# A graph layer on one core: h in two float32r parts instead of three bf16 parts, counts in a ring of three half blocks

## The chip, the cores and the metric

The kernel runs on one core of a Trainium2 chip. The metric is the device time of one execution in microseconds (us). The kernel before took 511.15 us (median of 3 runs, 510.1 to 515.61). The profiled execution took 511.06 us.

Engines are named as in the profile: PE is TensorE (PEld its weight loads), DVE is VectorE, ACT is ScalarE, POOL is GpSimd, SP is the engine whose queue issues most of the DMAs.

## The reference

There are 6250 nodes with 64 features and 206250 edges, sorted by their destination `dst`, with 64 features each. In short:

```python
h   = maximum(layernorm(x), 0)
msg = h[src] + edge_attr_64                      # one row per edge
agg = segment_sum(msg, dst, 6250)                # sum of the rows that end in a node
out = x + relu(agg @ W1 + b1) @ W2 + b2          # 64 -> 128 -> 64
```

Everything is float32. The matrix work of the last line is small; the cost lies in gathering `h[src]` and in summing by node.

## The kernel before

**Counting instead of gathering.** For most nodes no row of h is gathered. For each window of V = 3 neighbouring nodes, whose edges fit into 128 slots, the kernel builds two one-hot matrices on DVE (L702): `hot_lo` is the low 7 bits of each slot's source node, `hot_key` is the pair (which of the three nodes, which of HI = 49 high parts of the source). Their product on PE (L712) gives `pc`, the number of edges from each source to each of the three nodes. A step (`count`) does ST = 6 windows; the one-hots are built for two steps at a time. ACT (L714) copies 882 counts per partition from PSUM to `counts`, laid out as (high part, node). Steps are grouped in blocks of 14: 84 windows, 252 nodes. There are NW = 22 blocks and 310 steps, two of which hold NX = 12 second windows for nodes whose edges need more than 128 slots; these stand at the end of block SB = 8.

**The product with h.** The sum of h over a block's edges is 49 products over the high part: `h3[:, h]` (128 sources by their features) times `counts[:, h]` (128 sources by 252 nodes). h is held as three bf16 parts that add up to it. The first two are one 128-column matrix, so one matmul yields both (L747, the wide products); the third is 64 columns wide, and products of even and odd h go to the two halves of the array (L750, the narrow products). The two halves of the result, partitions 0 to 63 and 64 to 127, are added only in the layer, where W1 stands twice. `counts` has two buffers, one per block, so block b is multiplied while block b + 1 is counted (`multiply_to`): wide products in the steps of `wide_at`, narrow ones in those of `narrow_at`.

**Edge features.** Chunks of 42 nodes, two to a unit: `load` fetches a unit's rows (2 x 384 KB, SP's queue), `chunk_hot` builds its one-hots on DVE (L384), `chunk_sum` sums on PE into `bank` (L396), ACT copies it to `by_node` (L399) and then the fetch of the unit after the next is queued; `chunk_place` puts the 42 columns in their place in the block's `pv` (L408). A block has three units, summed at steps 3, 7 and 11 of the next block and placed at 7, 11 and 13.

**Gathered groups.** The edges of the last nodes are not counted: GP = 24 groups of 1024 edges. Their features are loaded, POOL adds rows of h to them by indirect DMA (eight a group, 192 in all, L256), and PE sums a pair of groups (L425, L429), 42 nodes wide; two adds on DVE (L418) bring it into `sums`.

**The layer.** `add_products` (L759) adds `pv` to `sums`. `mlp_hidden`, `mlp_product`, `mlp_add` and `mlp_store` do a block's two products and store it; x (with b2 added beforehand) is held whole in `xs`.

**Order.** All instructions are in an order written out by hand: the loop over steps puts the pieces above at fixed steps (`before`, `later`, `places`). Each engine works in order. When POOL's next gather is put into the order, and when a pair of groups is summed, follows a plan in us with the constants HEAD_US, STEP_US, GATHER_US, WORDS_US, OPENING_US. Two PSUM buffers hold `pc`, two SBUF buffers each the one-hots.

Of the kernel before, what the change touches and what calls it, by code (L numbers as in the profile page):

```python
# [11 lines left out]
I32 = mybir.dt.int32  # L12
I16 = mybir.dt.int16
# [24 lines left out]
W = 42  # L38
# [10 lines left out]
WR = 128  # L49
WR_BITS = 7  # L50
# [4 lines left out]
GP = 24  # L55
# [13 lines left out]
NX = 12  # L69
BT = 84  # L70
BN = V * BT
NW = 22
NWIN = NW * BT
# [3 lines left out]
SB = 8  # L77
DST_BITS = 13
# [8 lines left out]
assert NC * CN == NS and BN % CN == 0 and CV * V == CN and NX % ST == 0  # L87
# [9 lines left out]
HEAD_US = 1.7  # L97
STEP_US = 1.35
GATHER_US = 2.12
WORDS_US = 2.6  # L100
# [4 lines left out]
OPENING_US = 8.0  # L105
# [3 lines left out]
def gnn_kernel(ctx: ExitStack, tc: tile.TileContext, x, src_t, dst_t, dst_g, edge, w1, b1, w2, b2, out):  # L109
# [3 lines left out]
    start = [b * BN for b in range(NB)] + [N]  # L113
# [12 lines left out]
    agg = consts.tile([P, ACOLS], F32, name="sums")  # L126
# [5 lines left out]
    pools = [tc.tile_pool(name=n, bufs=1, reuse_waits="tile") for n in ("lists", "other")]  # L132
    pr = pools[0].__enter__()
# [10 lines left out]

    firstp_i = small.tile([1, GP], I32, name="firstp_i")
    nc.scalar.dma_start(firstp_i.rearrange("o (q h k) -> o q h k", h=2, k=1),
                        dst_g[GA // 2:G // 2, :, 0:1].unsqueeze(0))
    xl = consts.tile([P, HI + 1, D], F32, tag="x", name="xl")
# [19 lines left out]
    nc.scalar.activation(agg, zero.to_broadcast([P, ACOLS]), AF.Copy)  # L168
# [23 lines left out]
    edge_w = small.tile([P, 4], F32, name="edge_w")  # L192
    for k, of in enumerate((1.0 - W, 0.5, WQ - 0.5, SPAN - 0.5)):
        nc.gpsimd.memset(edge_w[:, k:k + 1], of)
# [16 lines left out]
    select = consts.tile([P, W], F32, name="select")  # L211
    nc.gpsimd.memset(select, 1.0)
    for q in range(JQ):
        part = select[q * QP:(q + 1) * QP, :]
        nc.gpsimd.affine_select(part, part, pattern=[[1, W]], compare_op=OP.is_equal, fill=0.0, base=-QS[q],
                                channel_multiplier=-1)
        nc.gpsimd.affine_select(part, part, pattern=[[0, W]], compare_op=OP.is_ge, fill=0.0, base=WQ - 1,
                                channel_multiplier=-1)
# [45 lines left out]
    def fetch_row(i):  # L264
        rows_of[i] = small.tile([P, L1], I32, name="rows", bufs=6)
        gather(rows_of[i], dst_g.rearrange("q h (r k) -> (q h r) k", k=L1), row_i[:, i:i + 1])

    def seek(i0, n):
        for i in range(i0, i0 + n):

            inrow = small.tile([P, L1], BF16, name="inrow", bufs=2)
            nc.scalar.activation(inrow, rows_of[i], AF.Sign, bias=nhalf[:, i:i + 1], accum_out=first[:, i, 1:2])  # L272
# [9 lines left out]
    dst_p = consts.tile([P, GP, J], I32, name="dst_p")  # L282
    rel_p = dst_p.bitcast(F32)
# [8 lines left out]
    def chunk_starts(c0, c1, tag="po", bufs=1):  # L292
# [6 lines left out]
        known["s", c0] = px  # L299

    def chunk_rows(c0, c1):
        px = known.pop(("s", c0))
        s = starts[:, c0:c1]
        nc.vector.tensor_scalar(s, px[:1, :c1 - c0], float(G * P * J - CE), None, op0=OP.min)
        nc.vector.tensor_copy(starts_i[:, c0:c1], s)

    def chunk_columns(t0, t1, tag="po", bufs=1):
# [12 lines left out]
        known["t", t0] = px  # L320

    def chunk_index(t0, t1):
        px = known.pop(("t", t0))
        nc.vector.tensor_copy(cols_i[:, t0:t1], px[:, t0:t1])

        nc.vector.tensor_scalar(cols[:, t0:t1], px[:, t0:t1], -float(CN), float(CN * EA), op0=OP.mult, op1=OP.add)
        if t0 == 0:
            nc.vector.tensor_copy(cols[:, NT:], px[:, NT:])
# [35 lines left out]
    assert sum(n for _, _, n in units) == NC  # L364

# [35 lines left out]

    def chunk_place(u):
        b, c, n = units[u]
        o = (NX * V if b == SB else 0) - start[b]
        of = by_node.pop(u)
        for i in range(n):
            a = (c + i) * CN + o
            nc.tensor.matmul(pvs[b][0][i * D:(i + 1) * D, a:a + CN], of[:, i, :], select, start=False, stop=False)  # L408

# [3 lines left out]
    def add_sums():  # L413
        for g, pa in to_add:
            for b in range(GB):
                done_at[g + b] = max(made)
                to = agg[:, ds(bases.pop(g + b), W)]
                nc.vector.tensor_tensor(to, to, pa[:, b, :], op=OP.add)  # L418
        to_add.clear()

    def sum_groups(g, tiles):
        pa = bank[:, :GB * W].rearrange("p (b w) -> p b w", b=GB)
        for b in range(GB):
            hot = work.tile([P, J, W], F32, tag="hot", name="hotp")
            nc.vector.tensor_tensor(hot, rel_p[:, g - GA + b, :].unsqueeze(2).to_broadcast([P, J, W]),  # L425
                                    iota[:, :W].unsqueeze(1).to_broadcast([P, J, W]), op=OP.is_equal)
            for j in range(J):
                k = j % 2 * D
                nc.tensor.matmul(pa[k:k + D, b, :], tiles[b][:, j, :], hot[:, j, :],  # L429
                                 start=(j < 2), stop=(j >= J - 2))  # L430
        sum_p = work.tile([P, GB, W], F32, name="sum_p", bufs=1)
        nc.scalar.activation(sum_p, pa, AF.Copy)
# [23 lines left out]
    def norm_center(k):  # L456
        h0, h1 = thirds[k]
        nc.vector.tensor_tensor(xh[:, h0:h1], xh[:, h0:h1], wide(mean, h0, h1), op=OP.subtract)
        part = counts[0].rearrange("p h n -> p (h n)").bitcast(F32)[:, h0 * D:h1 * D]
        part = part.rearrange("p (h d) -> p h d", d=D)  # L460
# [19 lines left out]
    def norm_h(k):  # L480
# [3 lines left out]
        nc.scalar.activation(h3[:, h0:h1, :D], xh[:, h0:h1], AF.Copy)  # L484

    def norm_b(k):
        h0, h1 = thirds[k]
        nc.vector.tensor_tensor(xh[:, h0:h1], xh[:, h0:h1], h3[:, h0:h1, :D], op=OP.subtract)
        nc.scalar.activation(h3[:, h0:h1, D:2 * D], xh[:, h0:h1], AF.Copy)

    def norm_c(k):
        h0, h1 = thirds[k]
        nc.vector.tensor_tensor(h3[:, h0:h1, 2 * D:], xh[:, h0:h1], h3[:, h0:h1, D:2 * D], op=OP.subtract)
# [12 lines left out]
    firstp = small.tile([1, GP], F32, name="firstp")  # L506
    nc.vector.tensor_copy(firstp, firstp_i)
    pe = ps.tile([P, GP], F32, tag="po", name="pe", bufs=1)
    nc.tensor.matmul(pe, ones[0:1, :], firstp, start=True, stop=True)
    nc.scalar.activation(row2[:, GA:], pe, AF.Copy)  # L510
# [20 lines left out]
    pools[0].__exit__(None, None, None)  # L531
    counts.append(ctx.enter_context(pools[1]).tile([P, HI, BN + NX * V], BF16, name="counts1"))
# [11 lines left out]
    b2s = consts.tile([NP, D], F32, name="b2s")  # L544
    nc.sync.dma_start(b2s, b2.partition_broadcast(NP))
    src_p = consts.tile([P, GP * J], I32, name="src_p")
    nc.sync.dma_start(src_p, src_t[:, GA * J:])
    nc.sync.dma_start(dst_p, dst_t.rearrange("p (g j) -> p g j", j=J)[:, GA:, :])

    def table_rows(index, tmp):  # L550
# [3 lines left out]
        nc.vector.scalar_tensor_tensor(index, index, float(HI), tmp, op0=OP.mult, op1=OP.add)  # L554

    def find_groups():

        nc.vector.tensor_scalar(base_i[:, GA:], row2[0:1, GA:], 0.0, float(N - 1), op0=OP.max, op1=OP.min)
        nc.vector.tensor_tensor(rel_p, dst_p, row2[:, GA:].unsqueeze(2).to_broadcast([P, GP, J]), op=OP.subtract)
# [46 lines left out]
    def turn_pair(i0):  # L606
        n = min(2, IC - i0)
        end = min(n * P, NWIN - i0 * P)
        mid = min(max(SB * BT - i0 * P, 0), end)
# [6 lines left out]
    def second_flags():  # L616
# [14 lines left out]
        return lambda: second_ranks(flag, prk, rank, one)  # L631

    def second_ranks(flag, prk, rank, one):
        nc.vector.scalar_tensor_tensor(rank, prk, 1.0, flag, op0=OP.add, op1=OP.mult)
        pick = late.tile([P, IC, NX], F32, tag="part", name="pick")
# [3 lines left out]
        px, pn = pxn[:, :2], pxn[:, 2:]  # L639
        for i in range(IC):  # L640
# [3 lines left out]
        return lambda: second_words(px, pn)  # L644

    def second_words(px, pn):
        second_i = small.tile([NX, 1], I32, name="second_i")
        nc.vector.tensor_copy(second_i, px[:NX, 1:2])
        nc.vector.tensor_scalar(second_b, px[:NX, 0:1], float(SPAN), None, op0=OP.subtract)
        nc.vector.tensor_scalar(second_n, pn[:1, :], float(DUMP), float(DUMP), op0=OP.add, op1=OP.min)  # L650
# [5 lines left out]
    bad = small.tile([P, 9], F32, name="bad")  # L656
    found = small.tile([1, 5], F32, name="found")

    def outside(k):
        over = late.tile([P, NWIN + NX], BF16, tag="part", name="over")[:, :GP * J]  # L660
        nc.scalar.activation(over, rel_p.rearrange("p g j -> p (g j)"), AF.Relu, scale=1.0 if k else -1.0,
                             bias=edge_w[:, 0:1] if k else 0.0, accum_out=bad[:, k:k + 1])

    def inside(n):
        which, k = divmod(n, 2)
        a = (keys[:, 1, :, 0], rel[:, :NC].rearrange("p c q k -> p (c q k)"))[which]
        over = late.tile([P, NWIN + NX], BF16, tag="part", name="over")[:, :a.shape[1]]
        nc.scalar.activation(over, a, AF.Sign, scale=-1.0 if k else 1.0,  # L668
                             bias=edge_w[:, (1, 3 - which)[k]:(2, 4 - which)[k]], accum_out=bad[:, n + 2:n + 3])

    def limits():
        nc.vector.tensor_reduce(bad[:, 6:9], bad[:, :6].rearrange("p (n k) -> p n k", k=2), AX.X, OP.add)
        nc.vector.tensor_tensor(needed, row2[0:1, GA:], needed, op=OP.is_lt)
        nc.vector.tensor_reduce(found[:, 3:4], needed, AX.X, OP.max)
# [484 lines left out]
```

## Time and profile before

| what | value |
|---|---|
| median of 3 runs | 511.15 us |
| profiled execution | 511.06 us |
| its span, first to last instruction | 509.4 us |
| mean granted TensorE clock | 0.991 |
| first eviction of counts starts | 42.0 us |
| first wide product starts | 63.0 us |
| last eviction of counts starts | 483.6 us |
| evictions (L714), mean of one | 310, 908 ns |
| wide and narrow products, mean of one | 1078 at 271 ns, 1078 at 274 ns |
| gathers on POOL, mean of one | 192, 1882 ns |

The span is the time from the first to the last instruction; the execution's time is 1.66 us longer. A matmul's duration in the profile reaches from its start to its modelled end, so neighbours overlap; what one costs in a row of matmuls is the distance of the starts.

### The profile page before, as it was taken

The page shows a single profiled execution, that of the slowest core. Times are in us where ns is not written, and L with a number is a line of the kernel's source. Part 1 is how long each engine was busy: PE and PEld are TensorE (multiplying, and loading weights), DVE is VectorE, ACT ScalarE, POOL GpSimd, SP SyncE. Part 2 cuts the span into 40 slices and gives each one's busy share as a digit, 9 for nine tenths or more (in the row PEclk, how much of TensorE's full clock was granted, in tenths as well). Part 3 has the DMA queues.
Part 4 walks back from the last instruction along what each step waited for, and adds up shares of the span by engine and source line. Part 5 has one row for each costly group of instructions (what it writes and reads, how often), then busy time and mean ns, then how long its engine had stood idle before and what let it go on. Part 6 is the DMA issues. An engine that isn't in the chain of part 4 may idle for free.

```text
span 509.4 us, 19099 instructions
## 1 busy us (share of the span) xinstructions
PE 442.5 (87%) x8183; PEld 380.9 (75%) x8184; DVE 416.8 (82%) x632; ACT 359.1 (71%) x530; POOL 412.0 (81%) x265
## 2 busy tenths in 40 slices
PE   1226678889999988989989999999999999999893
PEld 1115557778888877778878888888888988888782
DVE  4789999698999969979879879799698798698521
ACT  6648867678777656997757777767777777667611
POOL 6676888888874888889888888888888888898880
PEclk9999899999999999999999999999999999999997
DMA  8848722566686566565665676586675766846560
GB/s 235 250 127 276 204 31 59 118 166 165 170 219 188 141 153 161 140 144 163 146 173 108 145 191 145 147 191 147 152 188 144 194 148 140 200 105 153 118 146 17
DMA packets 113544, 79.04 MB, mean 155 GB/s; under 512 B 32920, under 2 KB 108686, under 8 KB 113230
## 3 DMA queue, kind: packets, MB, share of 16 engines
q1 hardware_dynamic: 83962, 65.99, 43.5%
q0 software_dynamic: 29200, 10.25, 17.0%
q10 hardware_dynamic: 292, 1.52, 1.0%
q8 instruction: 66, 1.08, 0.9%
q14 instruction: 24, 0.20, 0.1%
HBM read 73.74 MB, written 3.99 MB: 153 GB/s over the span
## 4 chain that ended last, share of the span: by engine, by line
PE 69%; DVE 17%; issue 4%; ACT 4%; DMA 3%; POOL 1%; DVEq 0%; ACTq 0%; POOLq 0%
PE pc L712 21%; PE pv L747 19%; PE pv L750 11%; PE bank L396 9%; DVE hot_key L702 6%; DVE hot_lo L702 5%; PE pv L408 3%; PE ph L799 2%; PE po L806 2%; PE bank L429 2%; ACT counts L714 2%; DMA rows<-in_dst_g,row_i 1%; DMA dstq<-in_dst_g,cols_i 1%; ACT over L668 1%; POOL rows L256 1%
## 5 line engine op out<-in xcount | busy, mean ns | idle before, releaser
L256 POOL DMA_INDIRECT pfeat<-table,src_p x192 | 361.4, 1882 | 61.3 <-issue 55.2
L714 ACT ACTIVATE counts<-pc 128x882 bf16<-128x882 f32 x310 | 276.8, 908 | 48.5 <-PE pc L712 33.9
L712 PE MATMUL pc<-hot_key,hot_lo 128*128 128x147 bf16 x1860 | 174.0, 231 | 25.8 <-DVE hot_key L702 13.8
L712 PEld LDWEIGHTS <-hot_lo 128*128 128x128 bf16 x1860 | 134.2, 99 | 49.3 <-DVE hot_key L702 18.1
L702 DVE TENSOR_TENSOR hot_lo<-iota_lo,keys 128x1536 bf16<-128x1536 bf16 x155 | 147.9, 954 | 26.6 <-PE pc L712 26.0
L702 DVE TENSOR_TENSOR hot_key<-iota_key,keys 128x1776 bf16<-128x1776 bf16 x155 | 167.0, 1078 | 0.0
L747 PE MATMUL pv<-counts,h 128*128 128x252 bf16 (+1 forms) x1078 | 147.8, 271 | 0.1
L747 PEld LDWEIGHTS <-h 128*128 128x128 bf16 x1078 | 98.7, 97 | 8.0 <-issue 0.2
L750 PE MATMUL pv<-counts,h 128*64 128x252 bf16 (+1 forms) x1078 | 75.4, 274 | 0.0
L399 ACT ACTIVATE by_node<-bank 128x128 f32<-128x128 f32 x66 | 18.4, 278 | 58.2 <-PE bank L396 58.2
L396 PE MATMUL bank<-feat,hot 128*21 128x64 f32 x3168 | 58.6, 223 | 0.7 <-DVE hot L384 0.7
L396 PEld LDWEIGHTS bank<-feat,hot 128*21 128x21 f32 x3168 | 47.2, 102 | 13.7 <-issue 10.7
L750 PEld LDWEIGHTS <-h 128*64 128x64 bf16 x1078 | 53.9, 111 | 3.3 <-issue 0.2
L384 DVE TENSOR_TENSOR hot<-rel,iota 128x504 f32<-128x504 bf16 x66 | 44.8, 679 | 6.4 <-PE bank L429 5.5
L425 DVE TENSOR_TENSOR hotp<-dst_p,iota 128x336 f32<-128x336 f32 x24 | 11.7, 504 | 17.4 <-PE bank L396 17.2
L256 POOL DMA_INDIRECT words<-packed,first_i x15 | 20.5, 1367 | 4.6 <-issue 3.7
L256 POOL DMA_INDIRECT rows<-in_dst_g,row_i x15 | 17.0, 1132 | 8.7 <-ACT inrow L272 3.0
L408 PE MATMUL pv<-select,by_node 128*64 128x42 f32 x264 | 21.1, 243 | 0.0
L408 PEld LDWEIGHTS pv<-select,by_node 128*64 128x64 f32 x264 | 13.2, 136 | 8.3 <-issue 0.6
L801 ACT ACTIVATE hid<-ph,b1s 128x252 f32<-128x252 f32 (+1 forms) x25 | 11.7, 466 | 8.4 <-PE ph L799 7.2
L759 DVE TENSOR_TENSOR sums<-sums,pv 128x252 f32<-128x252 f32 x22 | 9.0, 411 | 9.6 <-PE pv L750 9.6
L799 PE MATMUL ph<-sums,w1s 128*128 128x252 f32 (+1 forms) x50 | 15.4, 390 | 1.6 <-DVE sums L418 1.1
(172 smaller groups left out, 259.0 us busy)
## 6 DMA issues: line engine op xcount, KB each, us to landing
feat<-in_edge SPq DMA_DIRECT2D x132, 384.0 KB
pfeat<-in_edge SPq DMA_DIRECT2D x24, 256.0 KB
pfeat<-table,src_p POOLq DMA_INDIRECT x192
out_y<-y SPq DMA_DIRECT2D x24, 63.0 KB
xs<-in_x SPq DMA_DIRECT2D x4, 315.0 KB
dstn<-in_dst_g SPq DMA_DIRECT2D x1, 1024.0 KB
table<-xl SPq DMA_DIRECT2D x2, 512.0 KB
packed<-dstn ACTq DMA_DIRECT2D x1, 768.0 KB
```

What stands on the lines that cost most here:

```text
L256: nc.gpsimd.indirect_dma_start(out=rows, out_offset=None, in_=source, in_offset=bass.IndirectOffsetOnAxis(ap=index, axis=0), compute_op=op)
L384: nc.vector.tensor_tensor(hot_of[u][:, :n].rearrange("p c j w -> p (c j) w"), rel[:, c:c + n].rearrange("p c q k -> p (c q k)").unsqueeze( ...
L396: nc.tensor.matmul(bank[q * QP:q * QP + WQ, i * D:(i + 1) * D], hot[:, i, j, :], feat[i][:, j, :], start=(k == 0), stop=(k == JP - 1))
L399: nc.scalar.activation(by_node[u][:, :n].rearrange("p c d -> p (c d)"), bank[:, :n * D], AF.Copy)
L408: nc.tensor.matmul(pvs[b][0][i * D:(i + 1) * D, a:a + CN], of[:, i, :], select, start=False, stop=False)
L425: nc.vector.tensor_tensor(hot, rel_p[:, g - GA + b, :].unsqueeze(2).to_broadcast([P, J, W]), iota[:, :W].unsqueeze(1).to_broadcast([P, J, ...
L702: nc.vector.tensor_tensor(hot.rearrange("p t (m o) -> p t m o", o=2), iota_k.rearrange("p (m o) -> p m o", o=2).unsqueeze(1).to_broadcast( ...
L712: nc.tensor.matmul(pc[:, k, m * K:(m + 1) * K], hot_lo[:, j, :], hot_key[:, j, :K], start=True, stop=True)
L714: nc.scalar.activation(counts[b % 2][:, :, s * ST * V:(s + 1) * ST * V].rearrange("p h (k m) -> p h k m", k=2), pc[:, :, :ST // 2 * K].rea ...
L747: nc.tensor.matmul(pv, h3[:, h, :2 * D], of, start=(h == 0 and not clear), stop=False)
L750: nc.tensor.matmul(pv[k:k + D, :], h3[:, h, 2 * D:], of, start=False, stop=(h >= HI - 2))
L799: nc.tensor.matmul(ph[:, :n], w1s, agg[:, start[b]:start[b + 1]], start=True, stop=True)
```

## The change

- h is held as two float32r parts in `h2` (a rounded one and its remainder), side by side in 128 columns. Each block has 49 products of 252 columns; the narrow ones are gone. One residue pass (`norm_low`) replaces two.
- `counts` is float32r, in a ring of three half blocks of 126 nodes, 7 steps each. Block b lies in two of the three. Its products are done in steps 0 to 6 of block b + 1 (`PRODUCTS`), before step 7 writes into the first half's place. In every third block the halves lie in reverse order, and `column` and `add_products` allow for it.
- Units are summed at steps 7, 9, 11 and placed at 9, 11, 13; their one-hots are built two steps earlier. Layers start at steps 7 and 10 instead of 0 and 8.
- 23 blocks are counted (322 steps; NX = 14 second windows within block 8) and GP = 18 groups gathered. A group's edges are arranged by quarters of 32 partitions, so that a pair is summed as a unit is (21 nodes a quarter) and then placed by a computed selection, 52 nodes wide. A group's load is four DMAs instead of one.
- b2 is added by a one-row product; x is fetched block by block in `mlp_hidden`.
- `sums` is cleared by ACT in steps 15 to 21 rather than at the start. Several small results in PSUM are read by ACT rather than DVE.
- The plan's constants change.

```diff
-GP = 24
+GP = 18
+PQ = 4
+PK = J // PQ
-NX = 12
+NX = 14
-NW = 22
+NH = BN // 2
+NW = 23
-HEAD_US = 1.7
-STEP_US = 1.35
-GATHER_US = 2.12
-WORDS_US = 2.6
+HEAD_US = 1.5
+STEP_US = 1.2
+GATHER_US = 2.2
+WORDS_US = 2.9
-OPENING_US = 8.0
+OPENING_US = 3.0
...
-    h3 = consts.tile([P, HI, 3 * D], BF16, name="h3")
-    counts = [consts.tile([P, HI, BN + NX * V], BF16, name="counts0")]
+    h2 = consts.tile([P, HI, 2 * D], F32R, name="h2")
...
+        ring = ctx.enter_context(pools["ring"]).tile([P, 3, HI, NH], F32R, name="counts")
...
+    def norm_low(k):
         h0, h1 = thirds[k]
-        nc.vector.tensor_tensor(h3[:, h0:h1, 2 * D:], xh[:, h0:h1], h3[:, h0:h1, D:2 * D], op=OP.subtract)
+        nc.vector.tensor_tensor(h2[:, h0:h1, D:], xh[:, h0:h1], h2[:, h0:h1, :D], op=OP.subtract)
...
+    for q in range(PQ):
+        nc.tensor.matmul(pe[q * QP:(q + 1) * QP, 1, :], ones[0:1, :QP], firstp[:, :, q], start=True, stop=True)
+    nc.scalar.activation(row2[:, GA:], pe[:, 0, :], AF.Copy)
+    nc.vector.tensor_tensor(off_p, pe[:, 1, :], row2[:, GA:], op=OP.subtract)
...
+        half, i = divmod(s, STEPS // 2)
         nc.scalar.activation(
-            counts[b % 2][:, :, s * ST * V:(s + 1) * ST * V].rearrange("p h (k m) -> p h k m", k=2),
+            ring[:, (2 * b + half) % 3, :, i * ST * V:(i + 1) * ST * V].rearrange("p h (k m) -> p h k m", k=2),
             pc[:, :, :ST // 2 * K].rearrange("p k (m h) -> p h k m", h=HI), AF.Copy)
...
-        h = i % HI
-        of = counts[b % 2][:, h, :pv.shape[1]]
-        if i < HI:
-            nc.tensor.matmul(pv, h3[:, h, :2 * D], of, start=(h == 0 and not clear), stop=False)
-        else:
-            k = h % 2 * D
-            nc.tensor.matmul(pv[k:k + D, :], h3[:, h, 2 * D:], of, start=False, stop=(h >= HI - 2))
+        pv, done, clear = pvs[b]
+        a, z = sorted(((2 * b) % 3, (2 * b + 1) % 3))
+        of = ring[:, a:z + 1:z - a]
+        for h in range(done, upto):
+            nc.tensor.matmul(pv.rearrange("p (k n) -> p k n", k=2), h2[:, h, :], of[:, :, h, :],
+                             start=(h == 0 and not clear), stop=(h == HI - 1 and unplaced[b] == 0))
...
+        hot = work.tile([P, GB, J, WQ], F32, tag="hot", name="hotp")
...
+            for k in range(PK):
+                for q in range(PQ):
+                    j = q * PK + k
+                    nc.tensor.matmul(bank[q * QP:q * QP + WQ, b * D:(b + 1) * D], hot[:, b, j, :],
+                                     tiles[b][:, j, :], start=(k == 0), stop=(k == PK - 1))
...
+    def residual(b):
+        xs[b] = work.tile([NP, 2, D], F32, name="xs", bufs=3)
+        nc.sync.dma_start(xs[b][:pairs[b]], x[start[b]:start[b + 1], :].rearrange("(p k) d -> p k d", k=2))
...
+            nc.tensor.matmul(po[:pairs[b], k, :], ones[0:1, :pairs[b]], b2s, start=True, stop=False)
...
-        nc.sync.dma_start(parts_of[g].rearrange("p j d -> p (j d)"),
-                          edge[g * P * J:(g + 1) * P * J, :].rearrange("(p j) d -> p (j d)", j=J))
+            for b in range(PQ):
+                nc.sync.dma_start(parts_of[g][b * QP:(b + 1) * QP].rearrange("p (q k) d -> p q (k d)", k=PK), rows[b])
...
-    SUMS, PLACES = (3, 7, 11), (7, 11, 13)
+    SUMS, PLACES, LAYERS = (7, 9, 11), (9, 11, 13), (7, 10)
+    PRODUCTS = (5, 12, 19, 26, 33, 41, HI)
...
-        if s in (0, 8) and ready:
+        if s in LAYERS and ready:
             mlp(ready.pop(0), n)
```

More of the change, by code (lines that the diff above doesn't have):

```diff
@@ L37 @@
 GB = 2
-W = 42
+W = 52
 CN = 42
@@ L110, in gnn_kernel @@
     nc = tc.nc
-    start = [b * BN for b in range(NB)] + [N]
+    start = [b * BN - (NX * V if b > SB else 0) for b in range(NB)] + [N]
     pairs = [(start[b + 1] - start[b]) // 2 for b in range(NB)]
@@ L364, in gnn_kernel @@
     assert sum(n for _, _, n in units) == NC
+    unplaced = [sum(1 for unit in units if unit[0] == b) for b in range(NW)]
     def load(u):
@@ L413, in add_sums @@
     def add_sums():
-        for g, pa in to_add:
+        for g, placed in to_add:
             for b in range(GB):
                 done_at[g + b] = max(made)
-                to = agg[:, ds(bases.pop(g + b), W)]
-                nc.vector.tensor_tensor(to, to, pa[:, b, :], op=OP.add)
+                half = slice(b * D, (b + 1) * D)
+                to = agg[half, ds(bases.pop(g + b), W)]
+                nc.vector.tensor_tensor(to, to, placed[half, :], op=OP.add)
         to_add.clear()
-    def sum_groups(g, tiles):
-        pa = bank[:, :GB * W].rearrange("p (b w) -> p b w", b=GB)
-        for b in range(GB):
[L424 to L432, printed above, removed]
@@ new lines, in place_groups @@
+    def place_groups(g):
+        of = by_node.pop(("h", g))
+        placed = ps.tile([P, W], F32, tag="po", name="placed", bufs=1)
+        sel = work.tile([P, GB, W], F32, name="sel", bufs=1)
+        nc.vector.tensor_tensor(sel, iota_wr.unsqueeze(1).to_broadcast([P, GB, W]),
+                                off_p[:, g - GA:g - GA + GB].unsqueeze(2).to_broadcast([P, GB, W]), op=OP.is_equal)
+        for b in range(GB):
+            nc.tensor.matmul(placed[b * D:(b + 1) * D, :], of[:, b, :], sel[:, b, :], start=True, stop=True)
+        sum_p = work.tile([P, W], F32, name="sum_p", bufs=1)
+        nc.scalar.activation(sum_p, placed, AF.Copy)
@@ new lines, in gnn_kernel, with by_quarters @@
+    nc.sync.dma_start(src_s.rearrange("p g b k -> p (g b k)"), src_t[:, GA * J:])
+    dst_s = early.tile([GP * PQ, PK * P], I32, name="dst_s")
+    nc.sync.dma_start(dst_s, dst_g.rearrange("q h (r k) -> (q h r) k", k=PK * P)[GA * PQ:G * PQ, :])
+    src_p = consts.tile([P, GP, PQ, PK], I32, name="src_p")
+    def by_quarters():
+        px = ps.tile([P, PQ, GP, PK], F32, tag="po", name="psrcq", bufs=1)
+        rows = src_s.bitcast(F32)
+        for q in range(PQ):
+            for b in range(PQ):
+                nc.tensor.matmul(px[b * QP:(b + 1) * QP, q], ident[:, q * QP:(q + 1) * QP], rows[:, :, b, :],
+                                 start=True, stop=True)
+        nc.scalar.activation(src_p.rearrange("p g q k -> p q g k"), px, AF.Copy)
@@ L562, in gnn_kernel, with turn_groups @@
+    def turn_groups():
+        rel_s = known.pop("g")
+        pt = ps.tile([P, PK, GP * PQ], F32, tag="po", name="pgrp", bufs=1)
+        for k in range(PK):
+            nc.tensor.transpose(pt[:, k, :], rel_s[:, k], ident[:GP * PQ, :GP * PQ])
+        nc.scalar.activation(rel_p.rearrange("p g q k -> p (g q) k"), pt.rearrange("p k r -> p r k"), AF.Copy)
     behind = small.tile([P, IC], F32, name="behind")
@@ L630, in second_flags, with second_ranks @@
                              start=False, stop=(i == IC - 2))
[L631 to L635, printed above, removed]
+        nc.scalar.activation(rank, prk, AF.Copy)
+        return lambda: second_ranks(flag, rank, one)
+    def second_ranks(flag, rank, one):
+        nc.vector.scalar_tensor_tensor(rank, rank, 1.0, flag, op0=OP.add, op1=OP.mult)
+        pick = late.tile([P, IC, NX], F32, tag="dstq", bufs=2, name="pick")
         nc.vector.tensor_tensor(pick, rank.unsqueeze(2).to_broadcast([P, IC, NX]),
@@ L666, in inside @@
         a = (keys[:, 1, :, 0], rel[:, :NC].rearrange("p c q k -> p (c q k)"))[which]
-        over = late.tile([P, NWIN + NX], BF16, tag="part", name="over")[:, :a.shape[1]]
-        nc.scalar.activation(over, a, AF.Sign, scale=-1.0 if k else 1.0,
-                             bias=edge_w[:, (1, 3 - which)[k]:(2, 4 - which)[k]], accum_out=bad[:, n + 2:n + 3])
+        m = -(-a.shape[1] // CHECKS)
+        for i in range(CHECKS):
+            of = a[:, i * m:(i + 1) * m]
+            over = late.tile([P, 2 * CQ], BF16, tag="dstq", bufs=2, name="over")[:, :of.shape[1]]
+            at = bad[:, 4 + (which * CHECKS + i) * 2 + k:][:, :1]
+            nc.scalar.activation(over, of, AF.Sign, scale=-1.0 if k else 1.0,
+                                 bias=edge_w[:, (1, 3 - which)[k]:(2, 4 - which)[k]], accum_out=at)
@@ L805, in mlp_product @@
         for k in range(2):
[L806 removed]
+            nc.tensor.matmul(po[:pairs[b], k, :], ones[0:1, :pairs[b]], b2s, start=True, stop=False)
+            nc.tensor.matmul(po[:pairs[b], k, :], outs[b][:, k:2 * pairs[b]:2], w2s, start=False, stop=True)
         y = work.tile([NP, 2, D], F32, name="y")
@@ L876, in gnn_kernel @@
     load(1)
-    for g in range(GA + 2, GA + 4):
-        load_h(g)
+    open_ring()
     todo = {}
```

340 lines of the change are left out of this document (175 added, 165 removed).

## The prediction

> **What bounds the kernel now.** The page first: shares of the span, and the engines on the chain that ended last.
>
> ```profile
> PE 442.5 (87%) x8183; PEld 380.9 (75%) x8184; DVE 416.8 (82%) x632; ACT 359.1 (71%) x530; POOL 412.0 (81%) x265
> ...
> PE 69%; DVE 17%; issue 4%; ACT 4%; DMA 3%; POOL 1%; DVEq 0%; ACTq 0%; POOLq 0%
> ```
>
> An average over stages, so next the busy times by stretches of 40 us (columns: stretch, length, then PE, PEld, DVE, ACT, POOL, the granted clock, DMA share, GB/s).
>
> ```profile
> 160.00:200.00 40.00, 36.80 (x729) 31.75 (x721) 35.61 (x59) 26.12 (x40) 34.21 (x20) 1.00 0.68 171
> ...
> 280.00:320.00 40.00, 40.00 (x749) 35.07 (x747) 33.96 (x46) 30.58 (x45) 34.51 (x19) 1.00 0.69 165
> 320.00:360.00 40.00, 40.00 (x748) 35.11 (x746) 34.26 (x46) 30.28 (x46) 34.20 (x20) 1.00 0.69 165
> ```
>
> From 280 on TensorE has no idle time; VectorE has 15%, ScalarE a quarter. POOL's rest is the 0.3 us between gathers, so it too runs end to end. The timeline of one stretch gives what each PE piece costs: not its duration, which holds the drain, but from its start to the next start.
>
> ```profile
> 341.38 0.32 PE L408 MATMUL pv<-select,by_node 128*64 128x42 f32 x4
> ...
> 341.52 0.83 PE L750 MATMUL pv<-counts,h 128*64 128x252 bf16 x12
> ...
> 342.28 0.87 PE L396 MATMUL bank<-feat,hot 128*21 128x64 f32 x48
> ...
> 343.08 0.56 PE L712 MATMUL pc<-hot_key,hot_lo 128*128 128x147 bf16 x6
> ...
> 343.48 0.70 PE L747 MATMUL pv<-counts,h 128*128 128x252 bf16 x5
> ...
> 344.02 0.55 PE L712 MATMUL pc<-hot_key,hot_lo 128*128 128x147 bf16 x6
> ...
> 345.80 0.64 PE L799 MATMUL ph<-sums,w1s 128*128 128x252 f32 x2
> ```
>
> Placing 0.14, 12 narrow products 0.76 (63 ns each), a unit of edge features 0.80, five wide products 0.54 (108 ns each), a step's counting 0.40 and, up to the next start at 344.50, 0.48. The float32 product of the layer is two instructions, and the next start (346.27) is 0.47 later. A block of 14 steps: counting 14 x 0.44 = 6.2, wide 49 x 0.108 = 5.3, narrow 49 x 0.063 = 3.1, units 3 x 0.80 = 2.4, placing 0.4, layer 0.47 + 0.41 = 0.9, gathered groups 12 pairs x 1.06 / 22 = 0.6: 18.9 us. Measured from 280 to 400: 526 counting matmuls, at 84 a block 6.26 blocks, 19.2 us each. So 0.3 is switching, and the block's length is PE's sum.
>
> **The product.** The change drops the narrow products (3.1 a block) and replaces 49 wide bf16 ones by 49 float32r ones of the same 128x128 and 252 columns. No row has float32r. From below it costs what bf16 does, 108 ns; from above what float32 does, 0.47 us. I take 108: h is split in two parts of this type, which would be pointless if a product kept all of float32's digits; a type that needs a second part does not need float32's passes. A single instruction of the float32 pair (0.235) lies between and is a rival. The weights are four bytes wide too. The timeline of weight loads at a float32 transpose:
>
> ```profile
> 106.12 0.14 PEld L593 LDWEIGHTS pk<-ident,klo 128*128 128x128 f32 x1
> 106.19 0.14 PEld L594 LDWEIGHTS pk<-ident,khif 128*128 128x128 f32 x1
> 106.30 0.14 PEld L593 LDWEIGHTS pk<-ident,klo 128*128 128x128 f32 x1
> 106.41 0.14 PEld L594 LDWEIGHTS pk<-ident,khif 128*128 128x128 f32 x1
> ```
>
> They follow each other by 0.11 us with matmuls running beside them, so a wide float32 load just fits under 108 ns of streaming.
>
> **PE after, per block.** Counting 6.2, products 5.3, units 2.4, placing 0.4; the layer 0.9 plus the bias as two one-row products (four instructions, about 0.1 each as po's four take 0.41), times 25/23: 1.4; groups 9 pairs x (0.55 for 32 instructions at the units' 0.80/48, plus 0.14 for placing) / 23 = 0.3; switching 0.3. Sum 16.3, 2.9 under today's 19.2.
>
> **What is late next: VectorE.** Pairs of one-hots start 0.87 and 0.99 after each other in the chain of waits: 7 x 1.86 = 13.0 a block. Unit one-hots 3 x 0.6, add of products 0.33 (in a third of the blocks two adds: 0.4), layer add 0.25, groups 9 x (0.45 + 0.25 + 0.35) / 23 = 0.4: 15.9. So PE and DVE come out level and the halves of a block decide. The ring has three half blocks, so all products of a block must be done in the next one's steps 0 to 6, and units and layers move to 7 to 13. First half: PE 3.1 + 5.3 + 0.3 = 8.7, DVE 6.5 + 0.6 + 0.4 + 0.2 = 7.7. Second: PE 3.1 + 2.4 + 0.4 + 1.4 + 0.3 = 7.6, DVE 6.5 + 1.2 + 0.25 + 0.2 = 8.15. The larger of each: 16.85; the two one-hot buffers could even it out to 16.3. The eviction writes four bytes for two. ScalarE from PSUM takes 277 ns for 128 float32 elements and 908 for the 882 to bf16, 0.84 ns an element, and from SBUF 1063 to float32 against 1061 to bf16 for 1024: width costs nothing. Its block is 15 us (30.3 busy in two blocks), covered; without that cover it would cost what passes 16.9.
>
> **A transfer with less cover.** Units now lie at steps 7, 9, 11 instead of 3, 7, 11, and the third one's features are fetched when the first has been summed: four steps, 4 x 1.21 = 4.8 us. Today's such transfer, queue row and DMA windows:
>
> ```profile
> 342.87 1.00 SPq L375 DMA_DIRECT2D feat<-in_edge  x2
> ```
> ```profile
> 342.90:344.60 1.70, 1.70 (x41) 1.43 (x28) 0.94 (x2) 1.18 (x2) 1.40 (x2) 1.00 0.55 65
> 344.60:347.50 2.90, 2.90 (x39) 2.51 (x40) 2.89 (x4) 2.41 (x4) 2.60 (x2) 1.00 1.09 296
> 347.50:348.50 1.00, 1.00 (x14) 0.96 (x12) 1.00 (x2) 1.00 (x2) 0.69 (x2) 1.00 0.11 14
> ```
>
> The sum began at 342.28 and the bytes stop at 347.5: 5.2 us. A shortage of 0.4, of which DVE's longer second half hides some: 0.25. Block: 17.1. At the queue, each group's load becomes four issues (18 x 4 instead of 24, 0.36 each), and each layer fetches its rows of x; both stand before unit loads, which is the second rival.
>
> **Ends.** Counting begins at 42.0 (first eviction) and the first product at 63.0. In the head the clearing of the sums (5.54 on ScalarE until 9.58, with the cast of src right behind) goes, worth up to 3 us; the offsets' subtraction, which waits for ScalarE's copy of the first nodes, now stands before the two merges of dst, and copies through ScalarE are new: about as much. From -3 to +3, taken as 0. The clearing returns in steps 15 to 21, four times 1.4 us on ScalarE, which is busy 14.2 of 20 us there. From 63.0 to the last eviction's end at 484.5 lie 21 blocks in 421.5, 18 more than 21 x 19.2: lists unpacked, residues of h, second windows. Residues (one pass instead of two) and the b2 adds shrink, 4 us: 14 stay. The tail from 484.5 to 509.4 is 24.9; its narrow run (494.27 to 497.17) goes, and so does the wait for the last gathered nodes' layer (500.75 to 503.57), since 144 gathers of 2.2 us end some 100 us earlier; the last block's rows of x, fetched only at its layer, may come 2 us late: 21.
>
> Sum: 42 + 21 + 22 x 17.1 + 14 + 21 = 474 of span; the profiled execution's 511.06 stands 1.7 over its span, and at the median of 511.15. **476 us.** Own range 455 (blocks at 16.3, head -3) to 497 (blocks at 18).
>
> **Rivals.**
>
> 1. Slower: float32r streams at the pitch of one float32 instruction, 0.235. Place: the 49 products in steps 0 to 6. That half takes 3.1 + 11.5 + 0.3 = 14.9, the block 23.3, the tail 6 more: 42 + 21 + 513 + 5 + 27 + 1.7 = 610 (the early extras mostly hide under PE). It decides from a pitch of about 0.14: 35 us over 23 x 49 products. For it: four-byte rows cost this in every matmul shown. Against: the two parts. Chance 0.11.
> 2. The same place, with loads and streams in turn: 0.11 + 0.108 = 0.218, block 22.5, 591. Against: the five wide bf16 products above, on the same rows of the array, run at 0.108 with a load each. Chance 0.02. [...]
> 3. All of float32's passes: 0.47, block 34.9, 871. The split speaks against it. Chance 0.05.
> 4. The transfer is the bound: a pair of group loads (8 x 0.36 of issue, 512 KB at 296 GB/s, 4.7 us) stands before a third unit's features, seven times, and the 0.4 shows fully: up to 37 more, half likely, 497; the worst case, 513, is no change. For it: the queue works in order. Against: group loads come due anywhere in a block. Chance 0.15.
>
> POOL as the bound is out: 144 x 2.2 = 317 us from 60 on.
>
> **The numbers.** Forecast 0.67, rivals 0.11, 0.02, 0.05, 0.15. Within 1% (506 to 516, as little as a measurement here tells from none) fall 0.05 of the fourth; slower are the first three, 0.18; faster 0.77. The range runs from 450, as the head may give more, to 508, into the fourth case; what is left out is mostly the slow product.
>
> **What would show it.** Product pitch 108 ns in runs of 7; the counting phase near 1.22 us a step; PE under 97% and DVE over 93% between 150 and 430; no wait of the bank's matmuls on features above 1 us; evictions still at 0.91. A pitch over 0.14, or PE full in the first halves of blocks while DVE waits on pc, makes it wrong.

## The result and the profile after

The changed kernel took 542.25 us (median of 4 runs, 538.56 to 543.22) against 510.79 for the kernel before: a ratio of 1.058 with a 95% interval of 1.050 to 1.066. It is slower, outside the forecast's range and on the other side of no change.

The page of the changed kernel: engines' shares, then the engines and lines of the chain that ended last.

```profile
span 540.8 us, 17705 instructions
...
PE 457.6 (85%) x7459; PEld 399.0 (74%) x7460; DVE 419.5 (78%) x639; ACT 371.5 (69%) x582; POOL 333.9 (62%) x222
...
PE 63%; ACT 9%; POOL 7%; DVE 7%; issue 6%; DMA 5%; SPq 1%; DVEq 0%; POOLq 0%; ACTq 0%
PE pv L808 24%; PE pc L788 18%; PE bank L417 7%; ACT counts L791 6%; POOL pfeat L279 5%; PE po L857 3%; PE po L856 3%; DMA feat<-in_edge 3%; PE ph L849 3%; ACT over L743 2%; DVE hot_key L778 2%; PE pv L433 1%; DVE hot_lo L778 1%; DMA pfeat<-table,src_p 1%; POOL words L279 1%
```

PE has some 700 instructions fewer and is busy 15 us longer. Three stretches of 40 us (stretch, length, then PE, PEld, DVE, ACT, POOL, granted clock, DMA share, GB/s):

```profile
240.00:280.00 40.00, 33.69 (x465) 29.37 (x463) 30.25 (x53) 23.40 (x32) 34.08 (x20) 0.87 0.57 132
...
320.00:360.00 40.00, 38.84 (x647) 33.76 (x646) 31.76 (x43) 28.70 (x43) 25.52 (x14) 1.00 0.59 146
360.00:400.00 40.00, 39.48 (x641) 34.22 (x641) 31.57 (x44) 28.74 (x43) 26.96 (x15) 0.97 0.59 146
```

VectorE did not become the bound: between 320 and 400 it is busy 31.6 to 31.8 of 40 us, less than the 34 before, and PE is still nearly full. Between 150 and 430 PE is busy 93% of the time and VectorE 80%, where the forecast had under 97% and over 93%. The timeline of PE shows products in the first half of a block, then a placing and a layer in the second:

```profile
340.95 1.07 PE L808 MATMUL pv<-counts,h 128*128 128x252 f32 x7
...
341.86 0.56 PE L788 MATMUL pc<-hot_key,hot_lo 128*128 128x147 bf16 x6
...
348.03 0.32 PE L433 MATMUL pv<-select,by_node 128*64 128x42 f32 x4
348.31 0.87 PE L417 MATMUL bank<-feat,hot 128*21 128x64 f32 x48
349.11 0.43 PE L856 MATMUL po<-b2s,ones 1*126 1x64 f32 x2
349.46 0.44 PE L857 MATMUL po<-w2s,hid 128*126 128x64 f32 x2
349.84 0.43 PE L856 MATMUL po<-b2s,ones 1*126 1x64 f32 x2
350.20 0.44 PE L857 MATMUL po<-w2s,hid 128*126 128x64 f32 x2
350.52 0.56 PE L788 MATMUL pc<-hot_key,hot_lo 128*128 128x147 bf16 x6
```

Seven products from 340.95 to 341.86: 130 ns each, not 108. A placing, 348.03 to 348.31: 0.28 us for four instructions, where the kernel before took 0.14. The layer's second product with its bias, 349.11 to 350.52: 1.41 us, where the forecast had 0.8 and the kernel before took 0.41:

```profile
348.23 0.57 PE L806 MATMUL po<-w2s,hid 128*126 128x64 f32 x4
348.64 0.56 PE L712 MATMUL pc<-hot_key,hot_lo 128*128 128x147 bf16 x6
```

To see what the sum became, the distances from each PE start to the next were added up by line from 88 us to about the end of counting (516 after, where the last eviction ends at 514.8, and 484.4 before), idle time apart, and divided by the blocks in that time (20.7 after, 20.0 before):

| per block, us | before | forecast | after |
|---|---|---|---|
| counting | 5.9 | 6.2 | 6.2 |
| products with h | 8.4 | 5.3 | 6.6 |
| units | 2.4 | 2.4 | 2.6 |
| placing | 0.4 | 0.4 | 0.8 |
| closing product (L435) | none | not seen | 0.2 |
| layers | 1.0 | 1.4 | 2.1 |
| gathered groups | 0.6 | 0.3 | 0.4 |
| rest and PE's idle time | 1.1 | 0.3 | 1.8 |
| sum | 19.8 | 16.3 | 20.7 |

A few per cent of the records are missing, so the entries are good to some 0.1 us. The halves of a block differ: by the starts of counting on PE, in the seven blocks from 316 to 459 us the first half mostly takes 9.3 us, where the forecast had 8.7, and the second 10.4 to 12.1, where it had 8.15. Placing, closing and the layers stand in the second.

### The profile page after: what moved, and what is told of

Same layout as the page of the kernel before. It is cut to its first block, busy times and chain, and to the rows that moved or that the text cites. A ratio compares the mean times of both kernels' runs of the same rounds, so it can differ in the third digit from the quotient of the medians.

```text
span 540.8 us, 17705 instructions
## 1 busy us (share of the span) xinstructions
PE 457.6 (85%) x7459; PEld 399.0 (74%) x7460; DVE 419.5 (78%) x639; ACT 371.5 (69%) x582; POOL 333.9 (62%) x222
## 4 chain that ended last, share of the span: by engine, by line
PE 63%; ACT 9%; POOL 7%; DVE 7%; issue 6%; DMA 5%; SPq 1%; DVEq 0%; POOLq 0%; ACTq 0%
PE pv L808 24%; PE pc L788 18%; PE bank L417 7%; ACT counts L791 6%; POOL pfeat L279 5%; PE po L857 3%; PE po L856 3%; DMA feat<-in_edge 3%; PE ph L849 3%; ACT over L743 2%; DVE hot_key L778 2%; PE pv L433 1%; DVE hot_lo L778 1%; DMA pfeat<-table,src_p 1%; POOL words L279 1%
## 5 line engine op out<-in xcount | busy, mean ns | idle before, releaser
L791 ACT ACTIVATE counts<-pc 128x882 fp32r<-128x882 f32 x322 | 288.8, 917 | 80.7 <-PE pc L788 75.5
L279 POOL DMA_INDIRECT pfeat<-table,src_p x144 | 279.1, 1938 | 78.0 <-issue 38.7
L788 PE MATMUL pc<-hot_key,hot_lo 128*128 128x147 bf16 x1932 | 183.1, 235 | 26.6 <-DVE hot_key L778 13.0
L808 PE MATMUL pv<-counts,h 128*128 128x252 f32 x1127 | 175.6, 296 | 3.8 <-ACT counts L791 3.1
L808 PEld LDWEIGHTS pv<-counts,h 128*128 128x128 f32 x1127 | 146.5, 193 | 7.4 <-ACT counts L791 6.6
L405 DVE TENSOR_TENSOR hot<-rel,iota 128x504 f32<-128x504 bf16 (+1 forms) x69 | 46.6, 677 | 29.4 <-PE bank L417 27.4
L420 ACT ACTIVATE by_node<-bank 128x128 f32<-128x128 f32 (+1 forms) x69 | 19.3, 279 | 17.1 <-PE bank L417 16.2
L856 PE MATMUL po<-b2s,ones 1*126 1x64 f32 (+2 forms) x100 | 22.2, 303 | 1.2 <-ACT hid L851 1.2
L857 PE MATMUL po<-w2s,hid 128*126 128x64 f32 (+2 forms) x100 | 23.1, 314 | 0.0
L856 PEld LDWEIGHTS po<-b2s,ones 1*126 1x126 f32 (+2 forms) x100 | 15.2, 190 | 6.4 <-ACT hid L851 2.0
L849 PE MATMUL ph<-sums,w1s 128*128 128x252 f32 (+2 forms) x50 | 17.7, 436 | 1.9 <-ACT sum_p L476 0.8
```

What stands on the lines that cost most here:

```text
L279: nc.gpsimd.indirect_dma_start(out=rows, out_offset=None, in_=source, in_offset=bass.IndirectOffsetOnAxis(ap=index, axis=0), compute_op=op)
L405: nc.vector.tensor_tensor(hot_of[u][:, :n].rearrange("p c j w -> p (c j) w"), rel[:, c:c + n].rearrange("p c q k -> p (c q k)").unsqueeze( ...
L420: nc.scalar.activation(by_node[u][:, :n].rearrange("p c d -> p (c d)"), bank[:, :n * D], AF.Copy)
L788: nc.tensor.matmul(pc[:, k, m * K:(m + 1) * K], hot_lo[:, j, :], hot_key[:, j, :K], start=True, stop=True)
L791: nc.scalar.activation(ring[:, (2 * b + half) % 3, :, i * ST * V:(i + 1) * ST * V].rearrange("p h (k m) -> p h k m", k=2), pc[:, :, :ST // ...
L808: nc.tensor.matmul(pv.rearrange("p (k n) -> p k n", k=2), h2[:, h, :], of[:, :, h, :], start=(h == 0 and not clear), stop=(h == HI - 1 and ...
```

## The experiments

The experiments ran in three sets, each on one chip beside the kernel before, whose median was 514.6 us for the first four, 534.5 for the next four and 530.0 for the last two. So only ratios compare across sets. The changed kernel itself was not run again in these sets: that its ratio of 1.058 holds on the other chips is assumed, not shown.

**b2 on VectorE instead of PE.**

```diff
-            nc.tensor.matmul(po[:pairs[b], k, :], ones[0:1, :pairs[b]], b2s, start=True, stop=False)
-            nc.tensor.matmul(po[:pairs[b], k, :], outs[b][:, k:2 * pairs[b]:2], w2s, start=False, stop=True)
+            nc.tensor.matmul(po[:pairs[b], k, :], outs[b][:, k:2 * pairs[b]:2], w2s, start=True, stop=True)
...
+        nc.vector.tensor_tensor(y[:pairs[b]], y[:pairs[b]],
+                                b2s[:pairs[b]].unsqueeze(1).to_broadcast([pairs[b], 2, D]), op=OP.add)
```

> The changed kernel with b2 added on VectorE after the layer's add instead of by a one-row product on PE. Theory: PE paces the kernel, and the two one-row products of a layer cost it about 1.0 us (po took 1.41 us from its first start to the next piece's, against 0.41 before), so 25 layers give back 22 to 25 us: 515 to 522 us. Rival, VectorE paces it (it has 0.2 to 0.3 us a layer more here): 542 to 550.

525.42 us, 1.024 of the kernel before (1.016 to 1.031). Against the change's 1.058 that is 0.034, or 17 us, good to some 6 us by the two intervals: the direction of the theory, about three quarters of its size, in spite of one more instruction a layer on VectorE. PE paces the kernel, VectorE does not.

**The bias product with 128 rows.** Same instructions, other tile.

```diff
-ones[0:1, :pairs[b]], b2s, start=True
+ones[:, :pairs[b]], b2s, start=True
```

> The changed kernel with the one-row product of b2 done with 128 rows (ones times a matrix that holds b2 in its first row and zeros below), so the number of instructions stays and the switch between tiles of 1 row and of 128 rows goes. If the switch is the cost: po's eight instructions at about 0.1 us each, 0.85 for 1.41 us, 14 us less in all: 528 us. If the number of float32 instructions is the cost: po stays at 1.3 to 1.4 us, 540 to 543 us.

535.87 us in one run, 1.041. In the tally of starts an instruction of the bias product costs 124 ns instead of 183 and one of the layer's product beside it 129 instead of 174, which over the run comes to the same 9 us by which this run is shorter. So about half of the bias's cost (9 of 17 us, the first of these from one run) is changing between tiles of one row and of 128, and the rest is the four instructions.

**Products in bf16.** Type alone; h's third part is left out.

```diff
-    h2 = consts.tile([P, HI, 2 * D], F32R, name="h2")
+    h2 = consts.tile([P, HI, 2 * D], BF16, name="h2")
-        ring = ctx.enter_context(pools["ring"]).tile([P, 3, HI, NH], F32R, name="counts")
+        ring = ctx.enter_context(pools["ring"]).tile([P, 3, HI, NH], BF16, name="counts")
```

> The changed kernel with h's two parts and the ring of counts in bf16: the products have the same shape, the same halves and the same place, and h's third bf16 part is left out. Theory, four-byte weights set the pitch of the products: 131 ns falls to 108 to 112, 1.0 us a block: 515 to 520 us. Rival, the pitch comes from reading the two halves of the ring: it stays at 131, 540 to 543 us. If the width of what ScalarE writes counted, its eviction would fall from 917 ns.

527.96 us, 1.026 (1.019 to 1.034). The timeline of PE:

```profile
350.88 0.91 PE L808 MATMUL pv<-counts,h 128*128 128x252 bf16 x7
351.64 0.55 PE L788 MATMUL pc<-hot_key,hot_lo 128*128 128x147 bf16 x6
```

0.76 for seven: 109 ns, against 108 in the kernel before, whose counts of a block lie in one buffer, and 130 in the changed kernel. Reading the two halves of the ring costs 1 ns at most, the type 21. The time gained (0.032, 16 us) is less than 1127 x 21 ns = 24: second halves, where the bias stands, still took 10.4 us or more in most blocks after 270. From 88 us to the end of counting the granted clock also stood at half for 27 us in this run against 20 in the changed kernel's. Evictions: 909 ns against 917, so the width that ScalarE writes is 1%.

**Each product in two halves of 126 columns.**

```diff
-            nc.tensor.matmul(pv.rearrange("p (k n) -> p k n", k=2), h2[:, h, :], of[:, :, h, :],
-                             start=(h == 0 and not clear), stop=(h == HI - 1 and unplaced[b] == 0))
+            for k in range(2):
+                nc.tensor.matmul(pv[:, k * NH:(k + 1) * NH], h2[:, h, :], of[:, k, h, :], start=False, stop=False)
...
```

> The changed kernel with each float32r product split into two of 126 columns, same weights loaded twice (and one zeroing and one closing product of a block more, 4 us in all). If loading 128 columns of four-byte weights sets the pitch, 126 columns stay at about 131 ns: 98 of them take 12.8 us a block instead of 6.4, 680 us. If streaming sets it, 126 columns cost about 65 ns: 545 us.

663.95 us in one run. PE's timeline:

```profile
359.94 1.76 PE L809 MATMUL pv<-counts,h 128*128 128x126 f32 x14
361.54 0.56 PE L788 MATMUL pc<-hot_key,hot_lo 128*128 128x147 bf16 x6
```

114 ns for 126 columns. Half the columns save 16 of 130 ns, so most of the pitch does not go with the columns; what stays the same is the load of 128 columns of weights. PEld's rows are about as long as PE's distances: 0.89 us for the changed kernel's seven loads from 340.92, 1.64 for these fourteen from 359.91. That the load is the floor is argued from this and was not shown: no run changed the load alone. And 131 was not confirmed: 126 columns cost less than 252. Rival 2, load and stream in turn, stood at 0.218 us; 130 ns for 252 columns speaks against it.

**The removal alone, in the kernel before.** 47 of 49 narrow products go; the third part of h is left out for them.

```diff
-        else:
+        elif h >= HI - 2:
             k = h % 2 * D
             nc.tensor.matmul(pv[k:k + D, :], h3[:, h, 2 * D:], of, start=False, stop=(h >= HI - 2))
```

> The kernel before without 47 of the 49 narrow products of each block (the third bf16 part of h is left out for them; the last two stay and close the sum). It is the removal alone. By the prediction's step, PE falls by 3.0 us a block to 16.2 and VectorE is next at 15.9, so a block of 16.3 to 16.9: 22 x 2.3 to 2.9 us less and 2.7 less in the tail, 444 to 458 us. Rival, in-order waits of VectorE on PE take a good part of it: about 485 to 490.

529.77 us (528.01, 531.53, 533.15, 520.83) where the kernel before took 534.47 (529.57 to 539.69): about 1% less by the medians. Two of the four runs lie below all of the kernel before, the other two do not, so no size of a gain is settled; 444 to 458 and 485 to 490 were both missed. PE's waits (engine, line, waited for; us in total, times, longest):

```profile
PE bank L429 <- DMA pfeat<-table,src_p: 23.7, 17, 1.9
PE pc L712 <- DVE hot_key L702: 18.5, 16, 4.7
```

PE now waits for gathered rows, which it never did in the profile before; the last gather starts at 511.1 us (495.2 before). While the gathers kept up, the gain was there: the two blocks from 282 to 316 us took 17.4 and 16.7 us by the starts of counting, against 20.0 and 18.8 for the two from 284 in the kernel before, and the forecast's 16.3 to 16.9. Later three single gathers lasted 7.2 to 9.3 us, PE waited for their groups, and the granted clock was then at half for 10 us each time (from 396, 437 and 478); second halves there took up to 21 us. So the 192 gathers in a row stand about as close to bounding the kernel before as PE does; that fewer gathered groups, and with them a 23rd block, were needed for a larger gain is argued from this. The plan's STEP_US stayed at 1.35, so part of the waits may come from sums placed too early; that was not tested.

**Units at steps 3, 7, 11 again** (with b2 on VectorE).

```diff
-    SUMS, PLACES, LAYERS = (7, 9, 11), (9, 11, 13), (7, 10)
+    SUMS, PLACES, LAYERS = (3, 7, 11), (7, 11, 13), (7, 10)
```

> The kernel with b2 on VectorE, and the units summed at steps 3, 7, 11 and placed at 7, 11, 13 as in the kernel before (their one-hots still two steps earlier), so that each fetch of features has at least four steps with products in them and the last one eight. Theory, PE's waits for features (7.0 us) and the throttling of its clock after them are worth 8 to 15 us: 510 to 517 us where that kernel took 525. Rival, the pieces only move from one PE-bound half to the other: 522 to 528.

545.15 us, 1.018 (1.007 to 1.029), against 1.024 (1.016 to 1.031) with b2 on VectorE alone, on another chip. PE's wait for features is gone from its longest waits, and first halves grew from 9.3 to about 11 us; the intervals overlap. This fits the rival: the waits were real and worth little. The half clock did not go with them (14 us of counting from 88 on, against 17 with b2 on VectorE alone; the profiles' mean clocks are 0.965 and 0.961), so this run does not price it.

**Group loads from ScalarE's queue** (with b2 on VectorE).

```diff
-                nc.sync.dma_start(parts_of[g][b * QP:(b + 1) * QP]
+                nc.scalar.dma_start(parts_of[g][b * QP:(b + 1) * QP]
```

> The kernel with b2 on VectorE, and the loads of the gathered groups issued from ScalarE's queue instead of SP's. If eight group loads standing before a unit's features on SP are what makes PE wait, the wait goes: 513 to 520 us for 525. Rival, issuing on ScalarE holds back evictions by as much: 524 to 530.

572.27 us, 1.073 (1.065 to 1.081): worse than either expectation. ScalarE's waits, and one of its stretches of issuing:

```profile
ACT counts L791 <- PE pc L788: 63.0, 141, 1.3
ACT counts L791 <- DMA pfeat<-in_edge: 24.1, 5, 6.1
```
```profile
231.37 3.87 ACTq L879 DMA_DIRECT2D pfeat<-in_edge  x8
```

The loads held ScalarE up to 6.1 us at a time with evictions queued behind, and PE's two count buffers behind those: counting on PE waited 9.1 us for evictions, up to 3.2 at a time. The wait that the edit was aimed at did shrink: PE waited 1.6 us for features instead of 7.0. Within about 3 us of the end of each hold-up the granted clock went to half for 3.4 to 10.2 us; its mean in this run's profile is 0.898, in the changed kernel's 0.931.

**Both edits.**

> The two edits before this one together (units at 3, 7, 11; group loads from ScalarE's queue; b2 on VectorE). If both waits are separate: 506 to 514 us. If they are the same wait, as one of them alone: 512 to 518.

583.14 us, 1.095 (1.086 to 1.105). ScalarE's hold-ups (26.6 us in 6 waits) are the same, and nothing of the first edit offsets them.

**b2 on VectorE and bf16 products together.** The two diffs above; h's third part is left out.

> The two edits that each gave time back, together: b2 on VectorE, and h's two parts and the counts in bf16 (h's third bf16 part is left out). Alone they took the ratio to the kernel before from 1.058 to 1.024 and to 1.026. If they are separate pieces of one engine's sum, PE's: 0.99 to 0.995 of the kernel before, first halves of a block at 8.3 us and second halves at 8.5 to 10. Rival, VectorE becomes the bound at once (its block is 15.9 us of work without waits): 1.01 to 1.02.

518.15 us (514.18, 513.29, 522.12, 525.92), each below the fastest of the kernel before (530.04, 528.35 to 533.02, 7 runs); the ratio of the medians is 0.978, that of the two shorter runs 0.969, both without an interval. Alone the two edits gave 0.034 and 0.032; together 0.080 or more, at least their sum. Both are terms of PE's sum, one in each half of a block. Part of what goes beyond the sum may be the clock: it stood at half for 7 us of counting from 88 on here, against 17 and 27 with each edit alone. This version beats both kernels, but it keeps two bf16 parts of h instead of three, which is less than either holds.

**Work shared out again: 22 blocks, 26 groups** (with b2 on VectorE, float32r).

```diff
-GP = 18
+GP = 26
-NW = 23
+NW = 22
-STEP_US = 1.2
+STEP_US = 1.38
```

> The kernel with b2 on VectorE (float32r as in the change) and the work shared out again: 22 blocks counted and 26 groups gathered, STEP_US of the plan 1.38. PE has one block less (19 us) and four pairs more (4 us): 1.024 falls by 0.029 to 0.995 of the kernel before. POOL's chain of 208 gathers at 2.2 us from 45 on ends at 503, and the last pair's layer some 10 us later: about 515, 1.00. If POOL is not pressed by anything else: 0.995 to 1.005; if its gathers take longer under the denser traffic: 1.02.

558.48 us, 1.050 (1.043 to 1.058): 5% over the kernel before, where the worst expectation was 2%. The estimate of POOL's chain was too short. In the profile, which is of the longest of the four runs, the 208 gathers start from 47.0 to 542.9 us, 2.40 us apart on average, where the estimate took 2.2 and their end at 503. The 192 of the kernel before start from 44.8 to 495.2, 2.36 apart; by that pace the chain would have ended at about 535. PE waited 14.3 us for gathered rows. That this chain set the length of the run is argued, and no run with faster gathers tests it.

## Why the prediction was wrong

**What paces the changed kernel** is PE, as b2 on VectorE shows. The step that failed is the sum of PE's pieces after the change, 16.3 us a block, in the four terms below, and a fifth that the sum did not have: it took the clock as full. It measured 20.7. The mechanism that was forecast, PE falling under VectorE, did not come.

- **"I take 108."** The product is one instruction (1127 for 23 x 49; the layer's float32 product is two), as argued from the two parts, but it costs 130 ns. The reason given for the weights, that a load "just fits under 108 ns of streaming", came from float32 loads 0.11 apart beside matmuls that started as far apart; with float32r they do not fit (130 ns, and still 114 with half the columns). 22 ns x 49 is 1.1 us of the 4.4 by which a block is over; taking the type away gave back 16 us. Rival 1 had the right place and too high a pitch; its deciding point, 0.14, was worked out with every other term at its forecast value, so 0.13 could turn the sign once others gave way. That four-byte rows cost this "in every matmul shown" holds for the layer's float32 product (0.235 for 252 columns, 0.93 ns a column); the units' 48 in 0.80 us are 17 ns for 64 columns, 0.26 a column.
- **The layer, 1.4.** It is 2.1 a block: the bias was priced by the layer's own instructions (0.1 each), without what changing between tiles of one row and of 128 does to both neighbours. Taking it off PE gave back 17 us, shown; half of that lies in the tile.
- **Placing 0.4 and the close.** Placing is 0.8, since its cost from start to start includes what follows: before, that was a narrow product of the same 64-column tile. The removal alone shows it: in that run four instructions of placing took 138 ns where a narrow product still followed and 247 where a sum of features did, against 138 in the kernel before and 248 in the changed one. So part of the 3.1 that the narrow products "cost" came back. The extra closing product after the last placing, 0.2 a block, is in the diff and was not counted; it is read from the tally, and no run took it away.
- **"Switching 0.3".** Rest and idle are 1.8 a block against 1.1 before. Between 88 and 500 PE waited 9.9 us for one-hots (9.1 before) and 7.0 for features (none before). Between 260 and 265 it waited for features twice, 3.6 us in all, and the granted clock fell:

```profile
260.00:264.80 4.80, 1.22 (x38) 0.81 (x39) 3.04 (x5) 1.64 (x3) 3.90 (x3) 0.98 1.06 311
264.80:275.00 10.20, 10.20 (x80) 8.88 (x80) 4.12 (x6) 4.21 (x6) 8.66 (x6) 0.51 0.59 121
```

PE did 1.2 us of work in 4.8, and for the next 10 us ran at 0.51 of its clock. The second half of that block took 17.1 us. This is rival 4's mechanism (eight group loads stand at 253.11 in SP's queue, before unit loads at 258.29), in its place and with a clock penalty that it didn't have; over the run the waits themselves are worth little, by the units' experiment.

- **The clock, no term.** The first line is the kernel before, from its first product to the end of counting; the others are the changed kernel:

```profile
63.00:484.40 421.40, 401.74 (x7568) 347.77 (x7566) 361.41 (x523) 312.22 (x451) 355.82 (x194) 1.00 0.62 150
...
62.50:516.00 453.50, 416.73 (x6888) 366.16 (x6890) 367.42 (x535) 332.26 (x503) 285.59 (x158) 0.97 0.55 139
394.30:397.70 3.40, 3.03 (x30) 2.33 (x29) 1.17 (x2) 1.97 (x5) 0.00 (x0) 1.00 0.48 136
397.70:401.20 3.50, 3.50 (x22) 3.28 (x21) 2.78 (x6) 2.13 (x3) 2.51 (x2) 0.51 0.50 131
```

The 0.97 is five stretches at half clock (from 76.9, 220.2, 264.6, 309.0 and 397.7, 27 us in all). In those after 88 us PE's pieces took about 9 us longer by the tally than the same pieces elsewhere, 0.4 a block, which is spread over the rows of the table. What brings a stretch on is open: three follow 3.4 us (the length of the shortest stretch) in which PE was busy for 0.5 to 1.9, the other two 3.4 us in which it was busy for 3.0. No run set the clock apart.

Right were the first eviction and the first product (41.0 and 62.5 us, forecast 42 and 63: the head's gains and costs cancel), ScalarE's eviction (917 ns for 908), VectorE's own work (16.3 us a block between 280 and 400, forecast 15.9), and that POOL no longer bounds (its last gather starts at 430.5). The tail was 26 us, forecast 21: the narrow run is gone, but a layer now takes 1 us more, and the gathered nodes' last layer still came after the last block's, at half clock.

The sum of the shown pieces: with b2 on VectorE and bf16 products the ratio is 0.97 to 0.98, where the forecast 476 would be 0.93. The remaining 0.04 to 0.05 lies in placing, closing, waits, the clock and the tail, and is not divided by experiment.

Two small sums of the prediction are off as well: with blocks of 18 us its terms give 496, not 497, and half of rival 4's 37 us gives 495. Neither bears on the step that failed.

## What to carry to other kernels

Price an instruction by the distance to the next start in the order in which it will stand: here a type (130 ns against 109), a tile size (183 against 124) and a neighbour (placing, 138 against 247) each moved the cost, and the narrow lines, once removed, took only part of theirs away. When the sum is about to be level with a second engine, multiply each unmeasured term by its count first; here 22 ns at 1127 places and 1 us at 25 came to 25 us each by that count, and to 16 and 17 when they were taken away. And before forecasting a gain on one engine, check whether another (here POOL's 192 gathers) runs end to end beside it.

## What was not expected of the hardware

- A float32r product of 128 x 128 by 252 columns is one instruction with 130 ns from start to start; with 126 columns 114; in bf16 109 with 252.
- A product with one row beside one with 128 rows: 183 and 174 ns an instruction, against 124 and 129 where both have 128 rows.
- A placing of four instructions (64-column tile) took 138 ns where a product in a 64-column tile followed, 247 where a sum of features did.
- Between the first product and the end of counting, where PE is 92% busy, the changed kernel's granted clock stood at half in five stretches of 3.4 to 10.2 us, two of them right after 3.4 us in which PE was busy for 3.0.
- The same kernel before took 510.8, 514.6, 530.0 and 534.5 us (medians) in the four sets of runs, the last three on different chips.
